# Two lists of a kernel arranged anew: the order of its steps and the banks of its PSUM tiles

## The chip, the cores and the metric

The kernel runs on one core of a Trainium2 chip. A time is the device time of one execution in microseconds (us). The kernel before took 725.67 us, the median of three runs from 723.29 to 729.24. A core has a matrix engine, TensorE (PE in the profile, with its weight loads listed apart as PEld), the elementwise engines VectorE (DVE), ScalarE (ACT) and GpSimd (POOL), and a queue engine SyncE (SP) from which most transfers are issued. Each engine carries out its own instructions strictly in the order of the program and waits on semaphores for the others. Matmul results go to PSUM, which this kernel uses as eight banks of 128 x 512 floats.

## The reference

The input `x` has 4 sequences of 256 tokens with 256 features, all in float32. Eight blocks follow one another, each added to its input; `LN` is a layer norm without weights.

```
# first layer
x = x + time_mix(LN(x))       # token shift; k, v, r = mixes @ Wk, Wv, Wr; a scan over tokens with exp; (wkv * r) @ Wo
x = x + ffn0(LN(x))           # softmax over 8 experts, the best one: gate * (x @ W[e] + b[e])
x = x + state_space(LN(x))    # projection, causal conv of 4 taps, silu, chunked scan, gate silu, RMS norm, projection
x = x + ffn0(LN(x))           # the same expert weights once more
# second layer
x = x + attention_a(LN(x))    # 16 heads in 4 key/value groups, causal softmax
x = x + moe(LN(x))            # softmax over 32 experts, top 4, renormalized: sum_e w_e * (silu(x@g_e) * (x@u_e)) @ d_e
x = x + attention_b(LN(x))    # as above, with a linear position bias per head
x = x + moe(LN(x))
return x
```

## The kernel before

**Tiling.** The 1024 tokens are two groups of 512 (`x0`, `x1`), each four tiles of 128 tokens, and both groups stay on the chip throughout. Each group goes through the eight stages, and the two groups are interleaved: while one waits for a transfer, the other computes.

**Experts.** A router (`route_` L435, `route` L1043) normalizes, multiplies with the router weights (`pl`), finds each token's expert and its place there with comparisons on VectorE and small matmuls (`pr`). Then `send` writes every token's row to its expert's place in memory, with indirect transfers issued on POOL (L501, L1099); `fetch` reads the rows back by expert pair on SP; `turn` transposes them (PE `px`, ScalarE copies to `xT`). In the first layer `work` multiplies (`py`) and VectorE adds the bias (`ye`); in the second `gate` gives `pgu` (PE), silu `he` (ScalarE) and the product (VectorE, L1153), `turn_back` transposes it (PE `ph`, VectorE copies `hT`), and `down` gives `py` (PE) and `ye` (VectorE copy). SP stores `ye`; when all are stored, `back` gathers each token's rows on POOL (`yb`, L565, L1187) and `add` adds them to `x` on VectorE. Tile names end in group and number: `px_f00_1_3` is expert pair 3 of group 1 in the first expert stage; `f01` is its second pass, `f10` and `f11` the two of the second layer.

**Order.** Every part of a stage is a generator that issues some instructions and yields: a stream. `ORDER` lists, by hand-off, which stream takes its next step, and `follow` (L145) walks it. The engines' program orders follow from it, so the list alone says what each engine does first. In the list, capital letters are the first layer: `A0` and `A1` time mix (n norm, m mixes, k keys, v values, r receive, o output), `F0`, `F1` experts (r route, s send, w weights, f fetch, t turn, e work, b gathers, a adds), `S0`, `S1` state space (n norm, d time steps, c and h convolutions, g gates, m maps, u steps `au` on POOL, l decays `L`, v values, y, o, z what follows), `G0`, `G1` the experts again. Small letters are the second layer: `a`, `b` attention (n, k, q, v, p score maxima, w weights, c products, f finish), `e`, `f` experts (g gate, h turn back, d down). `x0` loads, `z0` stores, `la`, `lf`, `ls`, `ka`, `k1` and the like load and prepare weights. `br` (`breathe`, L219) issues one of 39 pauses on POOL, an operation on a spare tile.

**Banks.** `BANKS` gives each PSUM tile, in the order in which they are made, one of the eight banks; a tile waits until the last reader of the bank's previous tile is done.

**Table loads.** ScalarE's functions need a table set: exp is in set 0, ln in 5, silu in 18, and 6 holds exp and ln together. `act` (L226) keeps the loaded set in mind while the program is built, and puts a load ahead of a function that is not in it:

```python
        if sets and table[0] not in sets:
            table[0] = sets[0]
            nc.scalar.add_instruction(mybir.InstLoadActFuncSet(
```

So the order of the steps decides how many loads there are. The state space needs exp, ln and silu in turn, for the decays `L`, the time steps `dtln`, and the convolutions `cv` and gates `sg`.

Of the kernel before, what the change touches and what calls it, by code (L numbers as in the profile page):

```python
# [42 lines left out]
br*2 A0n kf x0 A0n x0 A0n x0 A0n x0 A0n ks A1n k1 A0n la*2 A0n lf A0n*3 lf A0n*2 ka x1 A0m0 A0n A1n  # L43
la x1*2 kf A1n*2 A0m1 x1 A0n A0m0 A0m1 cl lf A1n A0m0*2 k1 A1n*2 A0k0 A1n A0m2 A0k1 A1n A0k0*2 A0m2
A1n A0m1*2 cl lf la A0k0 cl A0k0 A0k1 ks A1n*2 A0k1*2 A1n A0m2*2 ks A0k0 A0k1 A1m0 A1n A0v1 A0v0 kf
A1m0 A0k0 A0m2 A1m0 A0k1 A0v0 A0v1 A0k0 A0r0 A0v0*2 A0k0 A1m0 A0k1 A0k0 A0k1 A1k1 A0k1*2 kf*3
A0v0*2 A1m2 A1k0 A0r1 A0v1*2 A1m1*3 A0v1 A0r0 la ls*2 A1k0 A0v1 l1 A1k0 ls A0r1 A1k0 A1k1 A0o A1m1
A1m2 A0o A1k1 A0o cl A0o*2 cl lf F0r*2 A0o F0r A0o*2 A1k0 lf cl A1m2 F0r*2 A1v1 A1m2 A1k0 F0r A1v0
F0r*2 A1k1*2 F0r*2 lf F0r A1v1 A1v0 F0r lf cl A1k0 F0r A1k1 F0r A1v0 A1k0 A1v0 lf A1k0 A1k1 F0r
A1k1*2 A1k0 F0r A1v1 F0r*3 A1m2 A1r0 A1r1 cl A1v0 A1v1 F0r A1v0 A1k1 A1v1*2 F0s A1r0 F0s A1r1 A1o  # L50
F0s A1o*2 F1r A1o F1r A1o F0s ks k1 A1o F0f*3 A1o F0t*2 F1r A1o F1r F0e F0t F1r F0f F1r*2 ks F0t
F1r*2 F0r F0t k1 F0e k1 ls F0e F1r cl F1r*3 F0t F0e*2 F1r F0e F1r ls F1r F0e cl F0t F1r F0e F0t
F1r*2 l1 F0e F1r F1s*3 l1 F0e*2 F1s F0e F1f F0w F0b*3 F0a F1f F1t F1f F1t*2 S0n F0a*2 S0n F0b S0n
F0a S0n PS F1e F1t S0n*5 F1e*3 k1*2 F1f F1t F1r S0n F1e S0n*2 F1t cl S0n S0h F1e S0h*2 F1e*2 S0h
F1w S0h F1t S0c cl S0c S0d F1t ks S0d*3 F1e*2 S0d*2 F1e*2 S0d S0c*2 S0u S0g S0c S0h S0g S0h*2 S0l
S0h*2 S0c F1b F1a S0h S0c*2 F1b S0h S0c S0l S0g S0c S0g S0c*2 S0g F1b S1n F1a S1n F1a F1b S1n S0h
F1a S0h S0m S1n S0u S0m S1n S0l S0h S1n S0g S0d S0h*2 S1n S0h S1n S0h S0l S1n*2 S0h*3 S0l*2 S0u S0g
S1n S0h S0l S1n*2 S0m S1c S0h S0m S0v*2 S0u S0l S0v S0u S0v k1 S0v S1c S0v k1 S0v*2 S1c*3 S0l cl
S1h S1d S0d S0v S1d S0v S0u k1 S0l br S0o S1h S0l*2 S0g S0y S1h*3 S0o S0l S1h S0o S1h*2 S1d S1h S0y
S1h*2 S0y*2 S0v S0l*2 S0o S1h S0o*2 S1h*2 S1c S0l S0z S1d S1h S1c S0v S0l S0u k1 S0z*2 S1d S1h S0z  # L60
S0l*2 S0z S1c S0l S0z S0l S1d S0z S1h S0o S0z S0y*2 S0z*2 S0u S0z*2 S1h S1g S1h S0z S1h br S0z S1g
S0z S0o S1c*3 S1d S1h S0l S1g S1c S0y S1h S0z S1h S0l*2 S0z*2 S1h S0z S0y S0z S1v G0r S1v S1u S1l
S1u S0z*3 S1m G0r S1u S1v S1u S1l S1d S0z S1v S1m S1v k1 S1v S1m S0z S1l S0z*2 S1u S1l S0z*3 S1v
S1l S1m S0z*5 S1u k1 S1d S0z G0r S0z S1l*2 S1y S1l S1v S0z G0r*2 br S1l*2 S1o S1y*2 S1l*2 S1y G0r
S1g G0r S1z G0r*2 S1z*2 S1g S1o G0r S1o G0r S1u G0r S1l G0r S1o G0r S1z S1v G0r S1g G0r S1o G0r S1g
S1l S1z S1u G0r S1z S1l S1z*2 G0r*2 S1l*3 G0s S1z G0s S1z G0s S1z*3 S1o G0s S1z*2 G0f S1g G0w S1o
# [12 lines left out]
a1p*3 a1w e0r a1w a1a e0r*5 lw e0r*3 a1p*2 e0r lw a1w a1p a1w a1p*2 e0r*2 lw e0s*2 a1b a1c lw a1p*3
a1b lw e0s a1f*2 a1w*2 lw a1p e0s a1w a1p a1w lw e0s a1p e0s a1p*2 a1w*2 lw e0s a1w a1p a1f a1w*2  # L80
a1f e0s a1p*2 e0s a1w a1f a1p a1c a1w*2 a1b a1w a1p a1w a1p*2 lw a1b a1f a1w a1p e0s a1w a1f e0s
a1p a1w a1c a1f a1w br a1w e0s*2 a1w e1r e0s a1w*3 e0s a1f a1w a1f a1b a1c a1f a1w a1f e0s a1b
a1w*4 a1f a1w*4 a1c a1w br a1w*2 a1f a1w*2 a1f a1w e1r e0f a1f e0t a1f a1w*3 a1c a1f e0t e0g e0f
a1f e0f a1f e0f a1f*3 e0t a1f e0g a1f e0g e0h e0t e0f e0t e0h e0f a1f*3 e0t e1r e0t e1r br e0g e1r
e0f e1r*2 e0d e0t e0g e1r*2 e0g*4 e0d e0t*3 e0f e1r*3 e0h br e0g e0d e1r e0t e0h*2 e0g e1r e0d e0f
e1r*2 e0g*3 e0d br e0d e0t e0h*2 e1r*2 e0t lw e0t e1r e0g*2 e0h e0t e0d e1r*2 e0g*2 e0h*2 br e1s*2
e0f e0g e0d e0w e1s e0t e0g br e0f e0t e0d e1s e0d e0g e0f e0g e0h e1s e0d*2 e0g*2 br e0t e0g e0d*2
e0h e0t e0f e0h e0g e0t e0g e0h e0d e0h e1s e0t e0d*2 e0f e1s e0g e0t e0g e1s*2 e0d e0h*2 e0d br
e1s*2 e0f e0g*2 e0d e1s e0d e1s e0h e0d e0g e0t e0d e0g e0h e0t e0d*2 e0t*2 e0g e0d*2 e0g*2 e0t*2
e0h e0d e0h*2 e0g*2 e0h e0d*3 e0t e0d e0h e0d e1s e0d e0g e0f e0d e1s e0g*2 e0h e0g e1s e0d e0g  # L90
# [1591 lines left out]
```

## Time and profile before

| | before |
|---|---|
| runs, us (median; all) | 725.67; 723.29, 725.67, 729.24 |
| profiled execution, us | 721.6 |
| its span, first to last instruction, us | 719.9 |
| mean granted PE clock | 0.950 |
| PE busy, us | 618.1 |
| VectorE busy, us | 470.6 |
| ScalarE busy, us, of it table loads | 270.1, 42.3 |
| POOL busy, us | 323.2 |
| moved by DMA | 94.02 MB, mean 131 GB/s |

The profile is of one execution, and 1.7 us of its time lie around the span. Busy time leaves out waiting. "PE px_f L536 <- DMA xe_f<-fsent: 10.8, 3, 8.6" means: PE, at the matmuls into `px_f` of line 536, waited 10.8 us in all, 3 times, 8.6 the longest, and what it waited for was the transfer that filled `xe_f` from `fsent`. Tile names in the profile leave out numbers. In the chain of waits a line is start, duration, and what ran or was waited for. The granted clock is TensorE's, 1.00 for full speed.

### The profile page before, as it was taken

Reading aid. Unit: us, or ns where it says so; the run is one execution under the profiler, and the core shown is the slowest. Engines: PE = TensorE matmul, PEld = TensorE weight load, DVE = VectorE, ACT = ScalarE, POOL = GpSimd, SP = SyncE. Lnnn points to the kernel's source line nnn. Section 1 sums busy time; section 2 is a strip of 40 time slices with the busy share of each in tenths; the row PEclk is TensorE's granted clock in tenths of the full one; section 3 lists DMA queues with packets and bytes.
Section 4 is the critical chain, followed back from the end, with each engine's and each line's share of the span. In section 5 each row is a group of like instructions: output and inputs, shape, how many; then the busy total and the mean of one; then the engine's idle time right before and its main releaser. Section 6 shows DMA issues by size and latency. Waiting matters only on the chain.

```text
span 719.9 us, 10090 instructions
## 1 busy us (share of the span) xinstructions
PE 618.1 (86%) x3184; PEld 418.0 (58%) x3184; DVE 470.6 (65%) x1511; ACT 270.1 (38%) x489; POOL 323.2 (45%) x371
## 2 busy tenths in 40 slices
PE   5679598989997999997999898998898899999910
PEld 2256464556676563453378887854444369889910
DVE  6986457768746587488537446768968737445732
ACT  4741127587442224422454232232442364223200
POOL 4114413536644414233842818407733851727644
PEclk9988889999998899998999999999999999999975
DMA  8932742000043143941246767512100242777743
GB/s 265 358 139 88 228 149 73 1 1 0 1 146 115 47 129 101 330 128 36 82 124 176 245 203 235 159 59 80 54 1 0 88 132 89 245 238 214 226 132 104
DMA packets 70828, 94.02 MB, mean 131 GB/s; under 512 B 6896, under 2 KB 60656, under 8 KB 70128
## 3 DMA queue, kind: packets, MB, share of 16 engines
q1 hardware_dynamic: 62944, 72.31, 31.5%
q0 software_dynamic: 7680, 20.98, 9.4%
q8 instruction: 27, 0.44, 0.3%
q14 instruction: 33, 0.27, 0.1%
q10 hardware_dynamic: 144, 0.01, 0.0%
HBM read 50.29 MB, written 42.99 MB: 130 GB/s over the span
## 4 chain that ended last, share of the span: by engine, by line
PE 51%; DVE 19%; POOL 8%; issue 8%; DMA 8%; ACT 4%; POOLq 0%; SPq 0%; DVEq 0%; ACTq 0%
PE pgu_f L245 7%; PE py_f L1171 5%; PE py_f L245 3%; POOL sent L1099 3%; DVE junk_a L917 3%; DMA yb_f<-done,bk_f 3%; DVE junk_b L917 2%; PE px_f L1135 2%; PE po_a L245 2%; PE pS_b L904 2%; PE pq_b L245 2%; PE pST_b L946 2%; PE pST_a L946 2%; PE pcv L245 2%; PE pS_a L904 2%
## 5 line engine op out<-in xcount | busy, mean ns | idle before, releaser
L245 PE MATMUL pgu_f<-gu,xT_f 128*128 128x192 f32 x512 | 93.7, 327 | 0.3 <-ACT xT_f L1139 0.3
L1187 POOL DMA_INDIRECT yb_f<-done,bk_f x64 | 65.6, 1025 | 60.3 <-DMA xe_f<-sent 16.0
L1099 POOL DMA_INDIRECT sent<-xn_f,to_f x64 | 63.3, 989 | 55.4 <-DVE he_f L1153 27.5
L245 PEld LDWEIGHTS pgu_f<-gu,xT_f 128*128 128x128 f32 x512 | 83.5, 190 | 2.1 <-ACT xT_f L1139 0.5
L1171 PE MATMUL py_f<-dw,hT_f 96*128 96x256 f32 x256 | 66.0, 382 | 3.7 <-DVE hT_f L1163 3.6
L1175 DVE COPY ye_f<-py_f 128x512 f32<-128x512 f32 x64 | 43.8, 686 | 25.3 <-PE py_f L1171 20.0
L917 DVE CUSTOM_DVE_ANT_0 junk_a<-pS_a,tri 128x128 f32<-128x128 f32 (+1 forms) x128 | 45.6, 356 | 18.1 <-PE pS_a L904 12.2
L917 DVE CUSTOM_DVE_ANT_0 junk_b<-pS_b,tri 128x128 f32<-128x128 f32 (+1 forms) x128 | 45.6, 356 | 13.2 <-PE pS_b L904 7.0
L1139 ACT COPY xT_f<-px_f 128x512 f32<-128x512 f32 x64 | 37.5, 585 | 41.6 <-PE px_f L1135 27.0
L236 ACT ACTIVATE he_f<-pgu_f 128x192 f32<-128x192 f32 x64 | 21.3, 333 | 83.7 <-PE pgu_f L245 75.2
L1171 PEld LDWEIGHTS py_f<-dw,hT_f 96*128 96x128 f32 x256 | 44.9, 190 | 11.2 <-issue 4.2
L1197 DVE SCALAR_TENSOR_TENSOR x<-yb_f,wt_f,x 128x256 f32<-128x256 f32 x64 | 31.4, 495 | 27.2 <-DMA yb_f<-done,bk_f 26.9
L221 POOL TENSOR_TENSOR gap<-gap,neghalf 128x4 f32<-128x4 f32 x39 | 42.6, 1091 | 0.9
L234 ACT ACT_TABLE_LOAD x33 | 42.3, 1283 | 0.6
L236 ACT ACTIVATE pT_b<-pST_b 128x512 f32<-128x512 f32 x48 | 26.3, 602 | 41.0 <-PE pST_b L946 35.9
L1135 PE MATMUL px_f<-ident,xe_f 128*128 128x128 f32 x256 | 38.0, 274 | 1.8 <-DMA xe_f<-sent 1.7
L236 ACT ACTIVATE pT_a<-pST_a 128x512 f32<-128x512 f32 x48 | 26.2, 600 | 31.3 <-PE pST_a L946 27.2
L957 POOL TENSOR_SCALAR_AFFINE_SELECT pT_b<-pT_b 128x512 f32<-128x512 f32 x32 | 20.8, 675 | 38.0 <-ACT pT_b L236 37.9
L1153 DVE TENSOR_TENSOR he_f<-he_f,pgu_f 128x192 f32<-128x192 f32 x64 | 22.2, 347 | 23.6 <-ACT he_f L236 23.5
L957 POOL TENSOR_SCALAR_AFFINE_SELECT pT_a<-pT_a 128x512 f32<-128x512 f32 x32 | 20.0, 643 | 32.3 <-ACT pT_a L236 32.1
L1163 DVE COPY hT_f<-ph_f 96x256 f32<-96x256 f32 x64 | 26.2, 414 | 12.4 <-PE ph_f L1160 11.0
L1135 PEld LDWEIGHTS px_f<-ident,xe_f 128*128 128x128 f32 x256 | 30.5, 141 | 5.2 <-issue 1.1
(295 smaller groups left out, 1321.7 us busy)
## 6 DMA issues: line engine op xcount, KB each, us to landing
xe_f<-sent SPq DMA_DIRECT2D x64, 256.0 KB, 3.3
done<-ye_f SPq DMA_DIRECT2D x64, 256.0 KB, 2.8
sent<-nil SPq DMA_DIRECT2D x16, 512.0 KB, 5.5
xe_f<-fsent SPq DMA_DIRECT2D x16, 256.0 KB, 3.0
fdone<-ye_f SPq DMA_DIRECT2D x16, 256.0 KB, 2.2
gu<-in_L1f_gate SPq DMA_DIRECT2D x4, 768.0 KB, 13.5
gu<-in_L1f_up SPq DMA_DIRECT2D x4, 768.0 KB, 17.1
dw<-in_L1f_down SPq DMA_DIRECT2D x4, 768.0 KB, 16.1
```

The lines of the kernel that those rows point to most:

```text
L221: nc.gpsimd.tensor_tensor(gap, gap, neghalf, ALU.pow)
L234: nc.scalar.add_instruction(mybir.InstLoadActFuncSet(name=nc.get_next_instruction_name(), act_func_set_id=sets[0], ins=[], outs=[]))
L236: nc.scalar.activation(dst, src, func, **more)
L245: nc.tensor.matmul(dst, w(c), rhs(c), start=(c == 0), stop=(c == n - 1))
L917: nc.vector.tensor_tensor_reduce(out=junk[:, :w], in0=both[r][:, at:at + w], in1=tri[:, S - w:], scale=1.0, scalar=NEG, op0=ALU.add, op1=A ...
L957: nc.gpsimd.affine_select(pT, pT, pattern=[[0, AG], [1, P]], compare_op=ALU.is_ge, fill=zero, base=0, channel_multiplier=-1)
L1099: nc.gpsimd.indirect_dma_start(out=sent_to[g][t * TOPK + j], out_offset=bass.IndirectOffsetOnAxis(ap=to[:, t, j:j + 1], axis=0), in_=xn[:, ...
L1135: nc.tensor.transpose(px[:, j * P:(j + 1) * P], xe[q][:, k, c * P:(c + 1) * P], ident)
L1139: nc.scalar.copy(xT[q].rearrange("p k c t -> p (k c t)"), px)
L1171: nc.tensor.matmul(py[:, k * D:(k + 1) * D], hT[q][:, k, :], dw[:, 2 * q + k, :], start=True, stop=True)
L1175: nc.vector.tensor_copy(ye.rearrange("p k d -> p (k d)"), py)
L1187: nc.gpsimd.indirect_dma_start(out=yb, out_offset=None, in_=done[g], in_offset=bass.IndirectOffsetOnAxis(ap=kept_["back"][:, t, j:j + 1], ...
```

## The change

`ORDER` and `BANKS` are replaced; nothing else is. Both orders hold every stream step the same number of times, and both end with the same stages interleaved in the same way. The instructions of each engine are the same but for the table loads, 34 in the program of before and 31 after; the three fewer are in the first layer (27 and 24). The pauses `br` stand elsewhere: the first two of before, at the very start, for instance. The weight loads at the start come in another order on SP. Line numbers after are two lower from L145 on. The whole lists are some 90 lines each; these are the start, the first expert stage into the state space, the beginning of the second layer's first experts, and the end:

```diff
 ORDER = """
-br*2 A0n kf x0 A0n x0 A0n x0 A0n x0 A0n ks A1n k1 A0n la*2 A0n lf A0n*3 lf A0n*2 ka x1 A0m0 A0n A1n
-la x1*2 kf A1n*2 A0m1 x1 A0n A0m0 A0m1 cl lf A1n A0m0*2 k1 A1n*2 A0k0 A1n A0m2 A0k1 A1n A0k0*2 A0m2
-A1n A0m1*2 cl lf la A0k0 cl A0k0 A0k1 ks A1n*2 A0k1*2 A1n A0m2*2 ks A0k0 A0k1 A1m0 A1n A0v1 A0v0 kf
-A1m0 A0k0 A0m2 A1m0 A0k1 A0v0 A0v1 A0k0 A0r0 A0v0*2 A0k0 A1m0 A0k1 A0k0 A0k1 A1k1 A0k1*2 kf*3
-A0v0*2 A1m2 A1k0 A0r1 A0v1*2 A1m1*3 A0v1 A0r0 la ls*2 A1k0 A0v1 l1 A1k0 ls A0r1 A1k0 A1k1 A0o A1m1
-A1m2 A0o A1k1 A0o cl A0o*2 cl lf F0r*2 A0o F0r A0o*2 A1k0 lf cl A1m2 F0r*2 A1v1 A1m2 A1k0 F0r A1v0
-F0r*2 A1k1*2 F0r*2 lf F0r A1v1 A1v0 F0r lf cl A1k0 F0r A1k1 F0r A1v0 A1k0 A1v0 lf A1k0 A1k1 F0r
-A1k1*2 A1k0 F0r A1v1 F0r*3 A1m2 A1r0 A1r1 cl A1v0 A1v1 F0r A1v0 A1k1 A1v1*2 F0s A1r0 F0s A1r1 A1o
...
-F1r*2 l1 F0e F1r F1s*3 l1 F0e*2 F1s F0e F1f F0w F0b*3 F0a F1f F1t F1f F1t*2 S0n F0a*2 S0n F0b S0n
-F0a S0n PS F1e F1t S0n*5 F1e*3 k1*2 F1f F1t F1r S0n F1e S0n*2 F1t cl S0n S0h F1e S0h*2 F1e*2 S0h
-F1w S0h F1t S0c cl S0c S0d F1t ks S0d*3 F1e*2 S0d*2 F1e*2 S0d S0c*2 S0u S0g S0c S0h S0g S0h*2 S0l
-S0h*2 S0c F1b F1a S0h S0c*2 F1b S0h S0c S0l S0g S0c S0g S0c*2 S0g F1b S1n F1a S1n F1a F1b S1n S0h
...
-e0f e1r*2 e0d e0t e0g e1r*2 e0g*4 e0d e0t*3 e0f e1r*3 e0h br e0g e0d e1r e0t e0h*2 e0g e1r e0d e0f
-e1r*2 e0g*3 e0d br e0d e0t e0h*2 e1r*2 e0t lw e0t e1r e0g*2 e0h e0t e0d e1r*2 e0g*2 e0h*2 br e1s*2
...
-f1d f0a f1h f0b f1d f1g*2 f1d*3 f0b f1g f1d f0b f1h*2 f1d f1h*2 z0*2 f0a f1d f0a f1d*5 f1b*2 f0a
-f1a*2 f0a f1b f1a f1b f1a f1b*2 f1a f1b f1a f1b f1a f1b*2 f1a f1b f1a f1b f1a f1b*2 f1a z1 z0 z1
-f1a*2 f1b f1a*2 f1b f1a z1*2
+A0n x0 A0n x0 A0n la x0 A0n x0 ka A0n*5 la A0n*2 ks A0n la A1n A0m0 x1*2 A1n lf x1 A1n l1 x1 lf A1n
+A0n A1n kf A1n ls*2 ks A0m0 A0m1*2 A0n A0m0 A0m2 A0m0 k1 br A1n A0m2 A1n A0k1*2 A1n A0m1 A0k0 A0m1
+A0v1 A0k0 A0k1 kf A0k0 A0k1 A0k0*2 A0v0 A1n A0k1 A1n A0m2 ls A0m2 A1n A0k0 A0k1 A1n A0m2 A1m0
+A0k0*2 A0v0 l1 cl k1 cl A0k0 kf A1n la A0r0 A0v0 A1m0*2 kf A0v1 kf A0k1 A0v1 A0k1 k1 br A0k1 A0r1
+A1m2 A0v1 A0v0 la A0k0 A1m0 A1k1 A0k1 A1m2 lf A0v0*2 lf*2 A0v1*2 cl A0r0 A0r1 A1m2*2 lf A1k1 cl
+A1m1 A1k0 A1m1 A0o A1k1*2 A1m1 A0o A1k0 A1m2 A1k0 A0o cl l1 A1k0 F0r A0o kf F0r A0o A1k0 A0o A1m1
+A0o F0r A0o F0r A1k1 F0r A1v1*2 A1k0 F0r*4 A1v0 A1k1 A1v1 A1k1 ls A1v0 F0r A1v0 F0r*2 lf*2 A1r0
+F0r*2 A1v0 A1k0 F0r A1k0*2 A1v0 A1k1 F0r*4 A1k1 A1r1 lf A1v1*2 A1k1 F0r A1k0 F0s A1v0 F0s A1v1 A1r1
+F0s A1r0 F0s A1o*2 F0f*2 F1r A1o*2 k1 A1o*3 F0t F0f*2 F0t F1r F0t F1r A1o ks F1r*2 F0w F1r ks F1r
+F0e F1r*2 F0e*2 F0t*2 F1r*4 ks*2 F0e F0t F1r F0t*2 F0e k1 F1r F0e*2 ls F1r*5 F1s F0e*2 F1s*2 F0e*2
+F1w F1s F0e F1f F0b*2 k1*2 F1t*2 F0b F1f F0a*2 F1f F1t S0n F0b F1f F1e S0n F0a*2 F1t*2 PS S0n*3 F1e
+S0n*4 cl*2 F1e*3 F1t S0n*3 F1t S0n F1t F1e S0h F1e*2 F0r S0d l1 F1e S0d S0h S0d F1e S0h cl*3 S0d
...
+e0t e0f a1f e0h*2 e1r e0g br e1r e0t*2 e1r*4 e0g*2 e0t e0g br e0g e1r e0d e0h e1r*2 e0h e0t e1r*2
+e0g e0f e0d e0g*2 e0d e0t e1r e0f e0g e0t br e0f e0h e1r*2 e0h e0g e0h e1r*3 e0g e0t e0f e0t e0d
...
+f1d*2 f0a z0*2 f1d f1h*2 f1g f1t f0b f1g f1h f1d f1t f1h f1d*2 f1g*3 f1d f0b f1h*2 f1g f1t f1d f0a
+f0b*2 f1d*4 f1h*2 br f1d*2 f1g*2 f1d f1g f1h*2 f1d*4 f0a f1d f0a f1b*3 f1a*2 f0a f1a f1b*2 f1a z0
+z1 f0a f1b f1a*2 f1b f1a f1b f1a f1b f1a f1b f1a f0a f1b*3 f1a*3 z1 z0 f1b z1 f1b f1a f1b f1a*2 z1
 """
...
 BANKS = """
-012345670124357602431576042317604231564720315672034651702365147203615207156047241635416704267536
...
+012345670123654701263547026157302615732601573601573601743560174506536537015347152074702136504271
...
 """
```

What a list does is seen better by tile. The order of PE's tiles from the first experts into the state space, before and after (without `pt_b0_0`, `pS` and `pe`):

```
before  py_f00_1_0 py_f00_1_1 px_f00_1_2 pcv_0_0 py_f00_1_2 px_f00_1_3 pcv_0_4 pd_0 py_f00_1_3 pg_0_0
        pcv_0_1 pcv_0_5 pg_0_1 pg_0_2 pcv_0_2 pG_0_0 pcv_0_3 pt_b0_1_0 pg_0_3 pt_b0_1_1 pG_0_1
after   py_f00_1_0 px_f00_1_2 py_f00_1_1 px_f00_1_3 pcv_0_0 py_f00_1_2 pd_0 py_f00_1_3 pg_0_0 pcv_0_4
        pcv_0_1 pcv_0_5 pg_0_1 pcv_0_2 pg_0_2 pg_0_3 pcv_0_3 pG_0_0 pG_0_1 pt_b0_1_0 pt_b0_1_1
```

And VectorE's from the logits of the first router to its counts, `mx_f00_0` to `up_f00_0` (`sb`, `sa` belong to the time mix of the other sequences):

```
before  mx_f00_0 ls_f00_0 sb_1_0 sa_1_1 key_f00_0 km_f00_0 oh_f00_0 up_f00_0*4
after   mx_f00_0 ls_f00_0 key_f00_0 km_f00_0 oh_f00_0 up_f00_0*4
```

Further places that the prediction speaks of: after, PE's list has `ph_f10_0_9` directly behind `pgu_f10_0_9`, `py_f10_0_15` directly behind `ph_f10_0_15` and `pgu_f11_0_14` directly behind `px_f11_0_14`, where before has other matmuls between each two. VectorE's list in the router of `f10_0` runs from `sel` to `up` without the attention's `junk` steps that stand between them before. `pyt_1_1_0` stands ahead of `py_f01_0_3` on PE, and two more `au` steps ahead of the four gathers of group 1's first `yb` on POOL.

## The prediction

> **What bounds the kernel now.** I read the busy table first, then the busy time by stage, the waits of TensorE (PE), the table of groups, and last the chain of waits around the largest stalls.
>
> ```profile
> span 719.9 us, 10090 instructions
> ...
> PE 618.1 (86%) x3184; PEld 418.0 (58%) x3184; DVE 470.6 (65%) x1511; ACT 270.1 (38%) x489; POOL 323.2 (45%) x371
> ...
> L234 ACT ACT_TABLE_LOAD x33 | 42.3, 1283 | 0.6
> ```
>
> PE's 618.1 us of matmuls are the same in both kernels, so the time is 618.1 plus what PE stands idle: 719.9 - 618.1 = 101.8 us. Only idle can be won or lost. ScalarE (ACT) is busy 38%, and 42.3 us of that are table loads, 1.283 us each.
>
> The same by stage (from:to, length, busy us of PE, its weight loads, VectorE, ACT, POOL; granted PE clock; DMA share; GB/s):
>
> ```profile
> 80.00:100.00 20.00, 9.83 (x41) 7.27 (x39) 7.80 (x26) 1.57 (x3) 9.38 (x10) 0.74 0.44 143
> 100.00:136.00 36.00, 33.11 (x105) 16.58 (x105) 27.06 (x62) 20.98 (x31) 15.51 (x25) 0.95 0.28 95
> 136.00:196.00 60.00, 58.06 (x289) 38.71 (x287) 46.69 (x90) 42.92 (x69) 29.66 (x33) 1.00 0.00 1
> 196.00:240.00 44.00, 37.21 (x187) 29.38 (x186) 26.94 (x81) 14.29 (x29) 18.98 (x20) 0.88 0.33 107
> ...
> 690.00:720.00 30.00, 0.00 (x0) 0.00 (x0) 8.14 (x17) 0.00 (x0) 16.10 (x16) 0.54 0.36 103
> ```
>
> PE's idle (length less its busy time): 10.2, 2.9, 1.9, 6.8 and 30.0 us. By the same view it is 14.6 before 40 us, 6.2 in 40-80, 2.0 in 240-320, 5.5 in 320-365, in the expert stages (365-480, 590-690) 7.0 and, without the tail, 3.3, in the second attention (480-590) 9.4. Note 136-196: ACT is busiest there, most loads fall there, and PE idles 1.9 of 60 us.
>
> What PE waited for, with total, times, longest:
>
> ```profile
> PE px_f L536 <- DMA xe_f<-fsent: 10.8, 3, 8.6
> ...
> PE pr_f L468 <- DVE j_f L475: 4.7, 1, 4.7
> PE pt_f L295 <- DVE xn_f L286: 4.4, 2, 3.6
> PE pr_f L1066 <- DVE up_f L1061: 4.1, 3, 2.8
> ...
> PE pg L245 <- ACT L L236: 1.8, 1, 1.8
> ...
> PE pG L678 <- ACT cv L236: 1.5, 1, 1.5
> ```
>
> Waits on ACT are small; the large ones are on VectorE and on round trips through memory.
>
> **The change part by part.** Both lists hold the same steps, so no arithmetic and no DMA is added or dropped; the order decides the table loads, 34 before (one ahead of the profiled span) and 31 after, all three fewer in the first layer. PE's order has the same stages at the same places, within some 6 us of PE work. "Cover" below is the PE work that a list puts between two matmuls, from mean durations of the profile. Eight places, each as PE idle after minus before:
>
> 1. *Head, to 64 us.* VectorE's steps from `mx_f00_0` to `up_f00_0` have other work between them in before (1.30 + 0.60 us, `sb`, `sa`), and `pr_f00_0` waits 4.7. After, they stand together, and `pr_1_0` (2.4 us of PE) fills in. But VectorE must do the same before `yT_1`: its steps from the last matmul they need to the second `yT_1` sum to 24.0 us over 15.3 of cover (8.7 short), before 26.2 over 17.4 (8.8 short). So `po_a0_1` is late next, by nearly as much. What I credit is the slow clock: eight `pr` matmuls took 6.05 us, 0.76 each, where the clock was 0.66 to 0.70, against a mean of 0.61, 1.2 in all. Taken -1.0; ends -4.7 (whole stall) and +1.0 (`mix0`, 0.7 later, and the second half of `yT`).
>
> 2. *First experts into the state space, 78-135 us.* The chain there:
>
> ```profile
> 109.02 1.28 ACT L234
> 110.31 0.01 issue
> 110.32 0.24 ACT dtln L236
> ...
> 111.07 0.63 DVE ye_f L553
> ...
> 111.73 2.19 DMA fdone<-ye_f
> ```
>
> `ye_f00_1_3` stands on VectorE behind a step that waits for `dtln`, and that for a load; then store, four gathers of 1.0 us, adds, norm, `pt_b0_1`. After, `pd_0` and `py_f00_1_3` come 1.9 us of PE work earlier (-1.9); `pG_0_0` moves 4.3 us back in PE's list, past its 1.5 us wait (-1.5); `px_f00_0_3` goes ahead of `py_f00_0_2`, whose 0.7 us wait on `xT_f` goes (-0.7). Against it, two more `au` steps of 1.06 us stand on POOL ahead of the gathers; the 2.19 us store hides some 0.8 of the 2.1 (+1.3). Taken -2.8; ends -4.9 (all idle that PE gathers there, 4.2, and the 0.7) and 0. The 8.6 us wait of `px_f00_1_0` stays: its cover is 2.7 us in both.
>
> 3. *Loads, 100-204 us.* 3 x 1.283 = 3.85 us less on ACT, but PE can gain at most the 1.9 it idles in 136-196, and one wait there, `pg` on `L` behind the load at 159.1, is 1.8 of it. Half of that: -0.9; ends -1.9 and +1.3 (one load newly on a path PE waits for). The Trainium skill, "ScalarE: Activation LUTs", section "What ACT_TABLE_LOAD costs", gives 1283 ns and a drain of about 1380 ns, 2.66 us a switch; by it, three loads would be 8.0 us of ACT, an estimate, and the term no larger, as PE's idle caps it. The rows above show no drain: the load ends at 110.30 and `dtln` starts at 110.32.
>
> 4. *Second pass of the first experts, 196-240 us.* The cover from `pr_f01_0` to `px_f01_0_0` falls from 11.25 to 10.36 us, so its 1.2 us wait on sends and fetch becomes 2.1 (+0.9). `py_f01_0_3` is 0.5 us later in PE's list, behind `pyt_1_1_0`, and an `x0` add and a statistics step (0.35 + 0.18) stand ahead of `xn` on VectorE, so the 3.6 us wait of `pt_f01_1` grows (+1.0). Taken +1.9; ends 0 and +3.6. The granted clock was 0.50 in 228-232, right after that wait. The Trainium skill, "TensorE: Matmul & The Clock Gate", section "Part 1: The HAM clock gate", halves the clock after an idle window of about 3.4 us; by it the 4.6 us stall would cost no second drop beyond the one already there, and a stall of 2 us none; the sum stays.
>
> 5. *First attention and its router, 300-365 us.* `sel` to `ch` on VectorE loses the attention maxima between them: `up_f10_0` is 0.9 earlier against the 2.8 us wait, and `qm` behind it 1.6 less short. But the norm of `f10_0` stands 2.1 us earlier in PE's list (short 3.2 instead of 1.25, +2.0), and `pt_a1_1` is newly short. Sums by VectorE's steps over cover come out about 1 us high where before can be held against its waits (1.8 where it waited 0.8). With the send span an estimated 1 us shorter (16 of 0.99 us, no pause between), +1.0; ends -3.5 (no new shortage is real) and +6.3 (the listed shortages, 14.5 against 8.2).
>
> 6. *Second experts, 365-480 and 590-690 us.* From `pgu` to `ph` PE needs `he` twice (0.33 + 0.35) and handovers, 0.85; from `ph` to `py` 0.41, 0.5; from `px` to `pgu` 0.59, 0.66. Cover is 0.00 after at `pgu_f10_0_9`, `ph_f10_0_15`, `px_f11_0_14`, 0.23 at `pgu_f11_0_6` and `ph_f11_0_13`; before nearly nowhere so little. Shortages: 3.6 after, 0.5 before, +3.1. If at each hand-over one `ye` copy (0.69) stands ahead on VectorE: 13.2 against 3.8, +9.4. The gathers of group 0 start about 1.3 us earlier and the adds stand later, which had held VectorE (1.5 and 0.8 us of PE's waits on `he` and `hT` fall on that); of it -0.6. Taken +2.5; ends -1.5 and +9.4.
>
> 7. *Second attention, 480-590 us.* Shortages 15.7 before, 14.4 after: -1.3; ends -4 and +4, half of the 9.4 idle.
>
> 8. *Tail.* Last gathers, adds and stores are the same; the last `ph` to `py` has cover 0 (before 0.91): +0.5; ends -0.5 and +1.0.
>
> Sum: -1.0 - 2.8 - 0.9 + 1.9 + 1.0 + 2.5 - 1.3 + 0.5 = -0.1 us. Against the profiled execution's 721.6 (span 719.9 and 1.7 around it) that is 721.5; against the median of the runs, 725.67, it is 725.6. I can't tell on which the next runs lie and take the middle, **723.5 us**.
>
> **The rivals.** *A, no change (0.39)*: gains of the first layer, -2.8 in all, are eaten by the second. For it: the largest idle (30.0 us tail, the 8.6 us wait, 14.6 at the start) isn't touched. Its own range is 718.4 to 732.9, 1% about the median, which is about what a measurement here can tell from no change.
>
> *B, faster (0.31)*: VectorE's order is what PE waits for, and the first layer and router come out at their good ends: -4.7 for -1.0, -4.9 for -2.8, -3.5 for +1.0, so -0.1 - 10.3 = -10.4, 713 us. For it: 4.7 + 4.1 us of waits on exactly those steps. Against it: VectorE's sum to `yT_1` is as short as before.
>
> *C, slower (0.30)*: one mechanism, hand-overs PE to VectorE to PE with less cover, in the router and the second experts: +6.3 for +1.0 and +9.4 for +2.5, so -0.1 + 12.2 = +12.1, 736 us. It decides once a `ye` copy stands ahead at most of the tight hand-overs. For it: PE idles only 10.3 us in the expert stages now, so there is little to win and a list with zero cover to lose by. Against it: five tight places among 64 tiles.
>
> *That fewer loads do nothing* is part of A: term 3 is then 0 and the sum +0.8.
>
> **How the numbers follow.** The half-widths of the eight terms, taken as independent, give 9.5 us about the sum; with 2 us for the base, and reaching B and C, the range is 711 to 738. Cases B and C are faster and slower by over 1% in nearly all of their chance: faster 0.31, within 1% 0.39, slower 0.30.
>
> **What would show it.** 30 table loads in the profile, ACT busy near 266; `pr_f` on `j_f` gone and `po_a` on `yT` waiting 3 to 5 us (term 1); `pG` on `cv` gone, `pt_b0_1` reached some 3 us earlier (2); `px_f` on `fsent` 11 to 12 us and `pt_f` on `xn_f` over 5 (4, 5); waits of `ph_f` on `he_f`, `py_f` on `hT_f` together 9 to 10 against 6.3 (6). It is wrong if the tail or the head moves by over 2 us, or if the second layer is better than before.

## The result

Four executions of the changed kernel took 731.47, 733.59, 735.55 and 736.97 us, median 734.57, beside four of the kernel before with median 724.85: ratio 1.0106, 95% interval 1.0058 to 1.0154. This first comparison says 1% slower. It did not come back. The same kernel was compared three times more, with twelve executions each time, on three chips: 1.0006 (0.9979 to 1.0034), 1.0003 (0.9969 to 1.0037), 0.9999 (0.9971 to 1.0026). Of these 36 executions one lies above 731.5 us. I therefore take the change as no difference, within 0.3%, and the first comparison as the thing to be explained; how far it can be is told below.

The profile of the first comparison (time 731.47 us, span 729.7 us), the lines that answer to those shown of before:

```profile
span 729.7 us, 10117 instructions
...
PE 623.4 (85%) x3184; PEld 422.6 (58%) x3184; DVE 471.2 (65%) x1511; ACT 266.2 (36%) x486; POOL 324.0 (44%) x371
...
L232 ACT ACT_TABLE_LOAD x30 | 38.5, 1283 | 0.5
```

Three loads fewer and 3.9 us less on ScalarE, as the list says; and 9.8 us more of span. PE is busy 5.3 us longer with the same matmuls, and idle 4.5 us longer. By stage (from:to, length, busy us of PE, its weight loads, VectorE, ScalarE, POOL; granted PE clock; DMA share; GB/s):

```profile
80.00:100.00 20.00, 9.62 (x43) 7.42 (x42) 9.80 (x34) 1.75 (x3) 9.47 (x10) 0.74 0.60 200
100.00:136.00 36.00, 34.56 (x121) 18.74 (x122) 24.88 (x56) 21.01 (x31) 13.05 (x17) 0.95 0.41 132
136.00:196.00 60.00, 59.95 (x302) 40.94 (x302) 51.45 (x108) 42.80 (x71) 33.47 (x46) 1.00 0.00 1
196.00:240.00 44.00, 32.11 (x158) 27.13 (x157) 20.79 (x62) 10.21 (x23) 14.00 (x13) 0.83 0.33 108
```

From 100 to 196 us PE now idles 1.5 us where it idled 4.8; from 196 to 240 it idles 11.9 where it idled 6.8. What PE waited for (total, times, longest):

```profile
PE px_f L534 <- DMA xe_f<-fsent: 14.4, 4, 9.6
...
PE pt_f L293 <- DVE xn_f L284: 7.6, 3, 6.3
PE pr_f L1064 <- DVE up_f L1059: 6.2, 3, 3.6
PE pST_a L944 <- DVE qm_a L929: 4.0, 2, 3.1
PE pr_f L466 <- DVE j_f L473: 3.2, 1, 3.2
...
PE ph_f L1158 <- DVE he_f L1151: 3.1, 5, 1.1
PE po_a L243 <- DVE yT L403: 2.9, 2, 1.5
...
PE pG L676 <- ACT cv L234: 1.3, 1, 1.3
PE py_f L1169 <- DVE hT_f L1161: 1.2, 3, 0.5
PE pY L746 <- ACT yfT L234: 1.2, 1, 1.2
```

To place gains and losses I took, for each PE tile, the end of its matmuls minus the PE work that the list puts up to it (mean durations of the profile of before). What this lag gains between two tiles that stand in both lists is PE's idle, and its slow clock, in that stage. Its increments in us, for the profiles at hand of the two kernels:

| stage, us from the start | term, as forecast | before (2 profiles) | after (4 profiles) | difference of means |
|---|---|---|---|---|
| 0-96, head and first experts | 1: -1.0 | 33.3, 33.8 | 34.1, 32.8, 34.1, 33.6 | +0.1 |
| 96-191, into and through the state space | 2, 3: -3.7 | 6.0, 6.9 | 0.5, 1.1, -0.7, 0.9 | -6.0 |
| 191-235, second pass of the first experts | 4: +1.9 | 8.1, 8.2 | 14.8, 16.2, 12.3, 14.6 | +6.3 |
| 235-361, first attention, router | 5: +1.0 | 6.9, 7.8 | 12.8, 6.1, 9.2, 7.2 | +1.5 |
| 361-483, second experts | 6, first part | 5.1, 5.1 | 1.9, 2.8, 1.7, 1.7 | -3.1 |
| 483-580, second attention | 7: -1.3 | 9.7, 11.3 | 11.4, 10.4, 11.1, 10.7 | +0.4 |
| 580-688, second experts again | 6, rest; in all +2.5 | 0.8, 1.1 | 3.1, 2.4, 3.8, 1.9 | +1.9 |
| tail | 8: +0.5 | 31.9, 32.1 | 33.0, 32.4, 33.1, 32.4 | +0.7 |
| sum | -0.1 | 101.8, 106.1 | 111.6, 104.3, 104.6, 102.9 | 1.9; without the first profile of after 0.0 |

Most increments repeat within a microsecond or two, so the larger differences between stages can be read although single executions scatter by 2 to 3 us (standard deviations of the three sets of twelve: 2.5, 3.1 and 2.3). What the list wins in the state space (-6.0) it loses in the next stage (+6.3), and what it wins in 361-483 us (-3.1) it loses in the stages behind (+3.0 in all). PE's busy time is not the same in all of them either: 618.1 and 621.4 us before, 623.4, 622.8, 619.7 and 620.7 after.

### The profile page after: what moved, and what is told of

Read it like the earlier page. It is cut to its first block, busy times and chain, and to the rows that moved or that the text cites. A ratio compares the mean times of both kernels' runs of the same rounds, so it can differ in the third digit from the quotient of the medians.

```text
span 729.7 us, 10117 instructions
## 1 busy us (share of the span) xinstructions
PE 623.4 (85%) x3184; PEld 422.6 (58%) x3184; DVE 471.2 (65%) x1511; ACT 266.2 (36%) x486; POOL 324.0 (44%) x371
## 4 chain that ended last, share of the span: by engine, by line
PE 52%; DVE 22%; issue 9%; DMA 6%; POOL 5%; ACT 4%; SPq 1%; another core or an unknown queue 1%; POOLq 0%; DVEq 0%; ACTq 0%
PE pgu_f L243 10%; PE py_f L1169 6%; DVE junk_b L915 4%; PE px_f L1133 3%; PE py_f L243 3%; PE pST_a L944 2%; PE pS_a L902 2%; PE pq_a L243 2%; PE pq_b L243 2%; PE pST_b L944 2%; PE ph_f L1158 2%; DVE cv L653 2%; DVE junk_a L915 1%; PE pctx_a L966 1%; PE pS_b L902 1%
## 5 line engine op out<-in xcount | busy, mean ns | idle before, releaser
L955 POOL TENSOR_SCALAR_AFFINE_SELECT pT_a<-pT_a 128x512 f32<-128x512 f32 x32 | 20.0, 639 | 33.3 <-ACT pT_a L234 33.2
```

The costliest lines, as they stand in the source:

```text
L955: nc.gpsimd.affine_select(pT, pT, pattern=[[0, AG], [1, P]], compare_op=ALU.is_ge, fill=zero, base=0, channel_multiplier=-1)
```

## The experiments

In the short diffs `old` and `new` stand for the two lists, written out step by step; a cut list takes its banks from the list that each step is from, moved where a bank would still be in use. Where the two lists have not done the same steps at a cut, each step is still done once, and the steps that are left follow in the order of the list that is named last. All ratios are to the kernel before on the same chip, each from 8 to 12 executions of the kernel.

**The changed kernel again.** No edit.

> The kernel after as it is, for a narrower interval and a second profile. Theory from the segments of five profiles (list of after against list of before): head +1.4, first experts to the state space -5.3, rest of the state space -0.7, second expert pass +7, first attention +1, first expert stage of the second layer -3.2, second attention and last stage +2, tail +1: 3 to 8 us slower than before. The stop of VectorE and ScalarE at 346 us should be missing in this profile if it was chance.

> The changed kernel a third time, unaltered, beside the three kernels below. Theory 'order' (the new lists cost about 1%, as in the first comparison): ratio to the kernel before 1.008 to 1.013, about 7 us. Theory 'scatter' (single executions of one list scatter by 2 to 3 us and the few first ones lay high): ratio 0.998 to 1.004. Theory 'chip' (the new lists lose on some chips and not on others): 1.008 to 1.013 on another chip than in the run that gave 1.0006, 1.000 on the same.

> The changed kernel a fourth time. So far 1.0106 (four executions of each), 1.0006 and 1.0003 (twelve each). Theory 'list' with the first comparison as the odd one: 0.998 to 1.003. Theory 'load' or 'chip': between 0.998 and 1.011, differing from the others by more than 0.003.

Measured: 1.0006, 1.0003 and 0.9999, each on another chip. Theory 'order' falls: the lists don't cost 1%. 'Chip' isn't supported by any of three chips; which chip the first comparison ran on is not on record. The page of the last:

```profile
span 721.0 us, 10117 instructions
...
PE 620.7 (86%) x3184; PEld 420.2 (58%) x3184; DVE 470.8 (65%) x1511; ACT 266.1 (37%) x486; POOL 324.4 (45%) x371
```

Same instructions, 8.7 us less span than in the first profile of the same kernel.

**The kernel before against itself.** No edit.

> The kernel before, unaltered, set against itself: what a comparison gives where there is nothing to find. Theory 'list' (a comparison's interval is to be believed, and the lists that came out slower are slower): ratio 0.997 to 1.003, its interval holds 1. Theory 'load' (each loading of a program has an offset of its own, of some tenths of a per cent, which all executions of that loading share): ratio off by 0.3 to 1.0% in either direction is to be expected, and the runs below don't repeat.

Measured: 1.0004 (0.9979 to 1.0030). This one, of twelve, is right within its 0.3%. On five chips the median of the kernel before lies between 722.62 and 726.67 us, 0.6% apart, more than the effect looked for: only runs of the same chip may be compared.

**The new lists up to a point.** Four cuts. At step 1637 both lists have done the same steps; at the other three, 8, 7 and 2 steps are done in one list and not yet in the other.

```diff
-ORDER = old
+ORDER = new[:535] + old[533:]      # first third
+ORDER = new[:795] + old[798:]      # to the first attention
+ORDER = new[:1129] + old[1131:]    # to the router
+ORDER = new[:1637] + old[1637:]    # to the second attention
```

> The lists of after up to the middle of the state space (PE tile pob_0_1, 166.6 us in the profile of after), the lists of before from there on. At equal PE work the profiles have after 2.1 us ahead at the first convolutions of group 1 and 4.7 ahead at the second router's pt_f01_0. Theory that leads carry: 2 to 4.7 us faster than before (720 to 723 us against 724.9). Rival, that the later waits on sends and fetches of the second expert pass eat any lead: within 1 us of before.

> The lists of after up to the first score maxima of the second layer's attention (254.0 us in the profile of after), before from there on. The profiles have after 2.4 us behind there. Theory: the loss of the second expert pass, 7.1 us from 4.7 ahead to 2.4 behind, is in this stretch of the lists, so 2.4 us slower than before and 4.5 to 7 slower than the first run of this set. Rival, that the late send and the long landing were chance in the one profile: no slower than before.

> The lists of after up to the projection po_a1_1_1 of the second layer's first attention (363.6 us in the profile of after), before from there on. The profiles have after 7.9 us behind there, of which 4.3 came in one stop at 346 us in which VectorE and ScalarE stood with no cause shown. If that stop belongs to the order: about 7.9 us slower than before. If it was chance in one execution: about 3.5 us slower.

> The lists of after up to the last tiles of the first expert stage of the second layer (487 us), before from there on; both lists hold the same steps at this cut. The profiles have after 4.7 us behind there, having won 3.3 in the expert stage with its tighter hand-overs. Theory: 4.7 us slower than before. Rival by my prediction's step on hand-overs: the expert stage costs 2.5 us or more, so slower than the run cut before it.

Measured: 1.0049 (1.0022 to 1.0077), 1.0103 (1.0068 to 1.0137), 1.0090 (1.0060 to 1.0120), 1.0012 (0.9979 to 1.0044). The first and the last fit neither of their theories. Taken alone the four would say that the loss is in the second pass and the first attention and won back by 1637. The traces say otherwise for the first two: the lag grows by some 5 us near the seam, where neither whole list has such a wait. The profile of the third is of one of its fastest executions (727.34 us, median 732.71), so where the others lose isn't shown. To tell a seam from scatter, one was run on another chip:

> The new lists up to step 795 and the old from there, a second time; the first gave 1.0103 [1.0068, 1.0137], the largest of all pieces, with a loss of 5 us at the seam in its trace. Theory 'list' (the seam's wait belongs to the list): 1.007 to 1.013 again. Theory 'load': 1.000 to 1.010, not the same.

Measured 1.0069 (1.0041 to 1.0096): it repeats, 5 us. Its first attention in the profile (waits of PE in 236 to 330 us), and the same stretch of before against itself:

```profile
PE pS_a L903 <- DVE nmx L916: 2.9, 1, 2.9
```

```profile
PE pST_a L946 <- DVE qm_a L931: 0.8, 2, 0.6
```

The wait of `pS_a` on the score maxima is there in both runs of the cut list, and not in the kernel before. So cutting a list makes waits that say nothing about either half. That it repeats, as the run below does, also speaks against an offset that belongs to each loading of a program. Only the exact cut can be read further, and with care: its lag in the second attention grows by 13.2 us, where the whole lists have 9.7 to 11.4.

**The second half alone.**

```diff
-ORDER = old
+ORDER = old[:1637] + new[1637:]
```

> The old lists up to the second attention (step 1637), the new ones from there: the complement of the run that had the new lists up to that point and gave 1.0012. The theory that the slower part is the second half (terms 6 late, 7 and 8): ratio 1.006 to 1.010. The theory that no half is slower by more than the scatter: 0.998 to 1.003. The prediction's terms for this part sum to about +0.3 us, ratio 1.000.

> The old lists up to step 1637 and the new from there, a second time; the first gave 1.0061 [1.0029, 1.0092]. Theory 'list': 1.003 to 1.009 again. Theory 'load': anything from 0.996 to 1.008, and with no offset 1.000.

Measured 1.0061 (1.0029 to 1.0092) and 1.0045 (1.0021 to 1.0069): the new second half is some 3 to 4.5 us slower, on two chips. Waits of PE in 480 to 690 us, this kernel and then the kernel before against itself:

```profile
PE pr_f L1065 <- DVE up_f L1060: 2.7, 2, 2.4
PE ph_f L1159 <- DVE he_f L1152: 1.9, 3, 1.1
PE pm_b L926 <- DVE nmx L916: 1.8, 1, 1.8
PE pST_b L945 <- DVE qm_b L930: 1.4, 4, 0.5
```

```profile
PE pm_b L927 <- DVE nmx L917: 3.4, 4, 1.6
PE pST_b L946 <- DVE qm_b L931: 2.6, 3, 1.2
...
PE ph_f L1160 <- DVE he_f L1153: 0.4, 1, 0.4
PE pr_f L1066 <- DVE up_f L1061: 0.4, 1, 0.4
```

The attention's own waits shrink from 6.0 to 3.2 us, and a wait of the router's rank matmul on VectorE, 2.4 us, comes in their place; in the last experts `ph_f` waits 1.5 us more. So the second half loses. By the stage table, without the first profile of after, it loses 2.6 us and the first half gains 2.7, before 191 us and in 361-483. That the first half alone is faster isn't shown: the exact cut gave 1.0012, and its longer second attention (13.2 us) takes back 2 to 3 us of the gain.

**The second pass of the first experts.** Two edits, each of a few steps. The clears of `sent` (three transfers of 512 KB from a tile of zeros) moved from right behind the store of `ye` to the end of group 1's work:

```diff
-a0k*2 cl G1s a0q a0v a0q cl G1s a0p*3 cl a0q*2 a0p G1s
+a0k*2 G1s a0q a0v a0q G1s a0p*3 a0q*2 a0p G1s
...
-G1t a0w G1e G1w a0c a0f G1e*2 a0p
+G1t a0w G1e G1w a0c a0f G1e*2 cl*3 a0p
```

> The kernel after with three of its 512 KB clears of the send buffer (steps cl, which SyncE issued at 220.6 to 222.9 us) moved behind the last store of the second expert pass of group 1. Theory that the clears hold up the gathers: the first gather lands 1.9 us sooner (4.8 becomes 2.9), so VectorE's first add comes at about 226 us instead of 228, and the time falls by 1.4 to 2 us against after. Rival, that the order on VectorE alone matters: the gather lands as late and the time is that of after.

and the four `xn` steps put ahead of the first two adds on VectorE:

```diff
-G0b*2 G1r G0b G0a a0n G1r G0a a0n G1r*2 G0r
+G0b*2 G1r G0b G1r*4 G0a a0n G0a a0n G0r
```

> The kernel after with the four normalizing steps xn_f01_1 of group 1 ahead of the first two adds of group 0 and their statistics on VectorE; the clears stay. Theory that the wait of the add for its gather is what group 1's norm pays: xn_f01_1 starts at about 226.8 us, when rstd is done, instead of 229.1, and is done by 228.2 instead of 231.8, so pt_f01_1 waits some 3 us less and the time is 2.5 to 3.5 us below after. Rival, that group 0's norm, now later, is waited for next: less than 1 us.

Measured 1.0002 (0.9976 to 1.0028) and 0.9979 (0.9950 to 1.0008). The stage to 235 us lost, beyond the round trip ahead of it, 10.3 us in all profiles of the new list, 8.6 with the clears moved and 7.05 with the norm first (before 7.4). First the new list (timeline: start, duration, engine, instruction, in brackets the idle time before it and its releaser), then the kernel before, the clears moved, and the norm first:

```profile
220.56 2.36 SPq L1463 DMA_DIRECT2D sent<-nil  x3
223.22 1.12 POOL L563 DMA_INDIRECT yb_f<-fdone,bk_f  x1 [4.38 <-DMA fdone<-ye_f]
...
228.03 0.48 DVE L572 SCALAR_TENSOR_TENSOR x<-yb_f,gate_f,x 128x256 f32<-128x256 f32 x1 [3.33 <-DMA yb_f<-fdone,bk_f]
...
229.64 0.45 PE L293 MATMUL pt_f<-ident,xn_f 128*128 128x128 f32 x1 [6.35 <-DVE xn_f L284]
```

```profile
223.87 1.12 POOL L565 DMA_INDIRECT yb_f<-fdone,bk_f  x1 [2.89 <-DMA fdone<-ye_f]
...
226.79 0.48 DVE L574 SCALAR_TENSOR_TENSOR x<-yb_f,gate_f,x 128x256 f32<-128x256 f32 x1 [0.53 <-DMA yb_f<-fdone,bk_f]
...
227.99 0.71 PE L295 MATMUL pt_f<-ident,xn_f 128*128 128x128 f32 x2 [3.60 <-DVE xn_f L286]
```

```profile
221.66 1.12 POOL L562 DMA_INDIRECT yb_f<-fdone,bk_f  x1 [4.34 <-DMA fdone<-ye_f]
...
224.55 0.48 DVE L571 SCALAR_TENSOR_TENSOR x<-yb_f,gate_f,x 128x256 f32<-128x256 f32 x1 [1.36 <-DMA yb_f<-fdone,bk_f]
...
226.16 0.30 PE L292 MATMUL pt_f<-ident,xn_f 128*128 128x128 f32 x1 [4.38 <-DVE xn_f L283]
```

```profile
226.65 1.61 DVE L283 TENSOR_SCALAR xn_f<-x,mv_f,rstd_f 128x256 f32<-128x256 f32 x4 [2.08 <-POOL rstd_f L237]
...
227.27 2.39 PE L292 MATMUL pt_f<-ident,xn_f 128*128 128x128 f32 x8 [4.09 <-DVE xn_f L283]
```

VectorE has the first add of group 0 in front of the norm of group 1, in both kernels; after, the add waits 3.3 us for its gather, and before 0.53. The gather was issued at 223.22 but landed late, the add starting 4.8 us behind it instead of 2.9: three clears went out on SP at 220.56 and for 4 us the DMA engines were full, as the first two rows show (share 0.99 and 1.00), the next two being before:

```profile
222.00:224.00 2.00, 1.29 (x6) 0.79 (x5) 1.80 (x7) 0.00 (x0) 0.78 (x1) 1.00 0.99 342
224.00:226.00 2.00, 0.00 (x0) 0.00 (x0) 0.63 (x3) 0.00 (x0) 1.67 (x3) 1.00 1.00 342
```

```profile
222.00:224.00 2.00, 2.00 (x11) 1.76 (x10) 0.48 (x1) 0.00 (x0) 0.13 (x1) 1.00 0.93 276
224.00:226.00 2.00, 0.39 (x2) 0.00 (x0) 1.49 (x5) 0.00 (x0) 1.70 (x2) 1.00 0.64 204
```

With the clears moved the add starts 2.9 us behind its gather again, and `pt_f` waits 4.4 us instead of 6.3; with the norm first, 4.1. Both edits so confirm the cause inside the stage: some 2 of the 2.7 us that `pt_f` waits longer than before are the clears. What they are worth to the whole is another matter. Of the 3.3 us that the norm-first edit takes out here, 1.2 come back at once, in the way that its rival names: `pt_a`, behind the norm of group 0, waits 1.2 us, which it doesn't in the new list. The times show some 2 us against the unedited list on the same chip (0.9979 beside 1.0006, the intervals overlap). With the clears moved the time didn't fall at all (1.0002): 3.5 us came back in 268-324 us.

**The good stages put together.** Three lists with the norm-first edit, and one made of pieces of both:

```diff
-ORDER = old
+ORDER = old[:231] + edited[233:736] + old[741:1131] + new[1129:1637] + old[1637:]
+ORDER = edited[:1637] + old[1637:]
+ORDER = edited[:2075] + old[2074:]
+ORDER = edited[:2075] + old[2074:]  # and the first `la` behind the fourth x0 tile
```

> Spliced lists: before up to px_f00_0_2, after to the second expert pass with xn_f01_1 ahead and its clears as spread as in before, before through the first attention of the second layer, after through its first expert stage, before to the end. If the segments add: state space -6 and +3.5 given back at the round trip of the sends, second layer's experts -3.2: 5 to 6 us faster than before (about 721 against 726.7). Rival, that splices and banks cost as much, as in the first of the spliced runs: within 2 us of before.

> The new lists up to step 1637 with the four xn steps of f01's second group moved ahead of the first two x0 adds (as in the run that gave 0.9979), the old lists from there. Theory that gains add up: the early half at 1.0012 and the edit at -0.0027 give 0.9985, and with the state space's -5 us kept and the router as in the new lists 0.995 to 0.999; the rival, that what is gained early is waited for again at a later round trip, gives 1.000 to 1.003.

> The new lists with the four xn steps of f01's second group ahead of the first two x0 adds, and from step 2075 (inside the second experts of group 1) the old lists. By the stages of the traces, the edit takes 3.3 us of PE's idle from the norm before f01's second half (7.05 for 10.33), and the old end 0.5 to 2 us from the last experts. Theory 'stages add up': 3 to 5 us faster than the changed kernel and the one before, ratio 0.993 to 0.997. Rival 'later waits take it back' (as in the run with the clears moved): 0.997 to 1.002.

> As the kernel beside it, and with the load `la` behind the fourth tile of x0 on SP's queue instead of ahead of the third and fourth. The first matmul is 0.9 us later in the changed kernel's traces than in the old's (8.8 against 7.9 us from the start). If that load is the cause, the first matmul comes at 7.8 to 8.1 us; if PE's lead is kept, 0.9 us less than the kernel beside it, ratio 0.992 to 0.996; if the first mixing waits for the weights instead, no difference.

Measured 0.9996 (0.9968 to 1.0025), 1.0001 (0.9964 to 1.0038), 1.0003 (0.9970 to 1.0036) and 1.0038 (1.0003 to 1.0072). None is faster than the kernel before. The theory 'stages add up' falls for such pieces. The profile of the last keeps the edit's shorter wait of `pt_f` (4.1 us), but has 12.1 us in the attention stage of 324-361 us where four others of the same steps have 6.5 (the pause told of below); and the list that is edited up to 1637 has 13.3 us in the second attention, a seam again. Its first matmul came only 0.3 to 0.4 us earlier, not 0.9, so the load is part of that delay at most.

**More table loads.**

```diff
-        if sets and table[0] not in sets:
-            table[0] = sets[0]
+        if sets and (again or table[0] not in sets):
+            table[0] = table[0] if table[0] in sets else sets[0]
...
-                act(L[k].rearrange("p h i l -> p (h i l)"), pS, AF.Exp)
+                act(L[k].rearrange("p h i l -> p (h i l)"), pS, AF.Exp, again=k % 2)
```

> The changed kernel with 8 table loads put in where none is needed, one ahead of every second Exp of a decay tile L in the state space (the table loaded already is loaded again): 10.3 us more on ScalarE, which PE waits on there only through L and cv. Prediction's reading (a load in the state space is mostly hidden, half of the 1.8 us wait was credited to three): 0 to +2 us against the changed kernel, ratio to it 1.000 to 1.003. The rival, a load counts in full on the path (what a search that places loads must assume): +10.3 us, 1.014. With a drain of its own at each switch, +16 to +21 us on ScalarE and gaps of over 1 us beside each load in the trace.

Three of the eight places needed a load anyway, so five were added, 6.4 us and not 10.3:

```profile
L232 ACT ACT_TABLE_LOAD x35 | 44.9, 1283 | 0.6
```

Measured 1.0039 (1.0005 to 1.0072) beside 1.0003 (0.9969 to 1.0037) of the unedited list on the same chip: +2.6 us, with an error a little larger than that. PE's busy time in 100-196 us falls by 1.7 us, and its waits on ScalarE there grow from 2.3 to 3.6 us (a new one of `pob` on `yfT`, 0.9). So by the waits a load on ScalarE costs PE about a fifth of its length, 1.3 of 6.4; by the times alone anything from nothing to nearly the whole is possible. At a fifth, three loads are worth 0.8 us, an estimate.

## What raised the first comparison

Its four executions lie 6 to 14 us above the later medians of the same kernel. Of the 9.8 us between the two first profiles, 2 us are the low profile of before (its second profile has a span of 724.2 us), and 4 to 5 us are a pause that this execution has at 346 us. VectorE, ScalarE and PE of the first profile of after, each from its own timeline:

```profile
350.92 0.69 DVE L929 TENSOR_TENSOR qm_a<-pm_a,qT_a 128x512 f32<-128x512 f32 x1 [4.91 <-remote]
```

```profile
351.69 1.08 ACT L234 ACTIVATE pT_a<-pST_a 128x512 f32<-128x512 f32 x2 [6.68 <-remote]
```

```profile
346.02 0.60 PE L925 MATMUL pm_a<-ident,nmx 128*128 128x128 f32 x4
346.55 1.13 PE L944 MATMUL pST_a<-qm_a,kb_a 64*128 64x512 f32 x4
```

and the same step in the second profile of the same kernel:

```profile
346.40 0.69 DVE L929 TENSOR_TENSOR qm_a<-pm_a,qT_a 128x512 f32<-128x512 f32 x1 [0.64 <-PE pm_a L925]
```

Both engines had PE results before them whose records end by 347.7 us, and went on some 4 us later, while POOL kept issuing its sends; "remote" says that the profile has no releaser. Of eleven profiles with the new steps there, VectorE stands 3.9 to 5.7 us ahead of a `qm_a` in six and at most 1.2 us in five; in three of the six the profile gives no releaser, in three it names a `pS_a` whose records end 1.4 us earlier. In the seven with the old steps no stop of VectorE at that place is over 2.7 us. The stretch from 324 to 361 us, where this pause falls, gains a lag of 6.5 us in four of ten profiles whose lists agree there, 8.2 to 9.8 in four and 12.1 in two. In those with the old list it is 8.1 in four of seven, 9.2 to 11.3 in the others. So the pause comes and goes with the execution, but is seen under the new steps alone: it may be a price of the new order that some executions don't pay. Its cause stays open, and so does why four executions in a row lay so high: the pause is at most half of it.

Two more things bear on it. PE's 5.3 us of longer busy time are a lower granted clock: 623.4 x 0.942 and 618.1 x 0.950 are the same 587.2 us. The four executions had 0.935 to 0.942, the three later sets 0.945 to 0.946 in the mean. The clock falls after stalls, as below, so this can follow from the pause as well as stand beside it; no run separates them. And three of the four executions of the kernel before were taken ahead of the comparison. If they ran on another chip, the medians of before on five chips allow some 2 us of the 10, an estimate.

## Why the prediction was right or wrong

The forecast was 723.5 us and no change as the likeliest case, with a sum of -0.1 us. The first measured median, 734.57, is inside its range of 711 to 738 and 1.06% above the kernel before, so outside the case. The later comparisons are inside it, and the sum of the stage table is +1.9 us, or 0.0 without the first profile. But the sum is right by terms that were wrong in opposite directions, which is luck.

Two steps failed. The first stands ahead of the terms: "PE's 618.1 us of matmuls are the same in both kernels" and "Only idle can be won or lost". PE's busy time was 619.7 to 623.4 us after, and 621.4 in the second profile of before; in the first comparison it is 5.3 of the 9.8 us. The second is term 4. In the first profile it is +6.6 instead of +1.9, and term 5, where the pause falls, +5.4 instead of +1.0; the pause has no term, and why it made the first four executions slow and not the later ones stays open. Term by term:

1. *Head, -1.0; +0.1.* That `po_a0_1` would be late next was right in direction: it waits 1.5 to 1.7 us where it waited 0.4. But all waits of `po_a` on `yT` fell from 4.0 to 2.9 us, below the 3 to 5 forecast, and `pr_f` waits 3.2 instead of none. Not priced: the first matmul is 0.9 us later and the long wait of `px_f00_1_0` is 9.1 to 9.6 us instead of 8.6; "its cover is 2.7 us in both" left out when the sends land.

2, 3. *State space and loads, -3.7; -6.0.* Right in sign and place, too small; `pt_b0_1_1` ends at 131.7 us instead of 134.4, though `pG` still waits 1.3 us. The two `au` steps that I charged with +1.3 cost nothing that can be seen. The loads are the smaller part, as forecast: `pg` on `L`, 1.8 us, is gone. On the drain that the Trainium skill, "ScalarE: Activation LUTs", section "What ACT_TABLE_LOAD costs", puts behind each switch at about 1380 ns: the row of 35 loads shows 0.6 us of idle before all of them, and after the load at 107.38 us the next load started at 108.92, with a function between; no run here shows it.

4. *Second pass, +1.9; +6.3, above its upper end of 3.6.* This is the term that failed. One step was "an `x0` add and a statistics step (0.35 + 0.18) stand ahead of `xn` on VectorE", priced at +1.0: that charges durations and nothing for a longer wait of the add, which stands ahead of `xn` in before as well and waits 0.53 us there. It waits 3.3 us after, since its gather lands behind clears that the list moved on SP and that I had not followed; `pt_f01_1` waits 6.2 to 6.3 us instead of 3.6 (forecast 4.6). The other step was the round trip, priced at +0.9 by its cover: `px_f01_0_0` waits 2.4 to 3.2 us for sends and fetch instead of 1.2 (forecast 2.1). First after, then the kernel before against itself:

```profile
PE px_f L534 <- DMA xe_f<-fsent: 3.2, 1, 3.2
```

```profile
PE px_f L536 <- DMA xe_f<-fsent: 1.2, 1, 1.2
```

Two things had no price. `pY` waits 1.2 us on `yfT` in all four profiles. And behind the longer wait of `px_f01_0_0` the clock falls: in the three profiles where it is 3.0 us or more, the granted clock is 0.50 for some 3 to 7 us right after it, 1.4 to 2.4 us of lag; behind the 2.4 us of the fourth, as behind the 1.2 us of before, it stays at 1.00. After the wait of `pt_f01_1` it is 0.50 in both kernels, so that longer stall brought no second drop, as forecast. The Trainium skill, "TensorE: Matmul & The Clock Gate", section "Part 1: The HAM clock gate", puts the drop behind an idle window of about 3.4 us; here the wait at this one place was enough in all nine profiles where it was 2.6 to 3.2 us, in four of six at 1.8 to 2.4, and in none of five at 0.9 to 1.3, so shorter waits than the page's sufficed.

5. *First attention and router, +1.0; +1.5, or +0.2 without the profile with the longest pause.* By the least disturbed profiles, 324-361 us is 1.6 us better (6.5 against 8.1).

6. *Second experts, +2.5; -3.1 and then +1.9.* The stage of f10 is better by 2.3 to 3.4 us in all four profiles of the new list: its waits `py_f` on `hT_f` and `ph_f` on `he_f` went from 4.3 to 2.3 us, those on `sent` and `up_f` (2.2) are gone. Waits of PE in 365 to 485 us, the kernel before against itself and the last run of the new list:

```profile
PE py_f L1171 <- DVE hT_f L1163: 2.3, 3, 1.2
PE ph_f L1160 <- DVE he_f L1153: 2.0, 2, 1.4
```

```profile
PE ph_f L1158 <- DVE he_f L1151: 1.8, 3, 0.8
PE py_f L1169 <- DVE hT_f L1161: 0.5, 1, 0.5
```

Places without cover didn't cost the hand-over that I summed. Where they did cost is f11, `ph_f` on `he_f` 1.1 us more. `ph_f` and `py_f` wait 4.3 us in all, not 9 to 10. The forecast had named "the second layer is better than before" as a sign that it is wrong; in 361-483 us it is.

7. *Second attention, -1.3; +0.4.* The shortages of the attention's own steps did shrink, by 2.8 us, and a wait on `up_f11_0` of 2.4 us took their place, as the second-half run shows twice.

8. *Tail, +0.5; +0.7.*

Rival C, hand-overs with no cover, isn't what made the first result slow: in its profile the two expert stages together differ from before by -1.0 us. Nor did case B's good ends for VectorE's order come in the head. The most that any list here gained was 0.2% (the norm first), and that interval holds 1.

## What to carry to other kernels

In a list that orders several engines, a step holds up what stands behind it on its engine until its own wait ends: price it by that end and not by its duration, and follow every bulk transfer that moved, even one that nobody reads soon. A lead won ahead of a round trip through memory is in part waited for again at it, and a list cut in two makes waits at the seam; cut where both halves have done the same steps, and even then look for such waits. And where executions scatter by 2 to 3 us in 725, four of each may not be enough to tell 1%, as here: run the kernel before against itself, and repeat on another chip, before looking for a cause.

## What the runs showed of the hardware

A pause in which VectorE stands 3.9 to 5.7 us, and ScalarE with it, behind results of PE whose records have ended: at one place of the program, in six of eleven profiles with the new steps there and in none of seven with the old; in three of the six no releaser is recorded. Clears of 512 KB hold back gathers behind them: three of them took the DMA engines to a share of 0.99 to 1.00 for 4 us, and the first add that waits for a gather started 4.8 us after the gather was issued, 2.9 us in the kernel before and with the clears moved. At one wait of PE (`px_f01_0_0`) over twenty profiles, the granted clock fell to about half behind all nine waits of 2.6 to 3.2 us, four of six of 1.8 to 2.4 and none of five of 0.9 to 1.3. The same kernel's median differs by up to 0.6% between five chips.
